# Sixteen of 52 pairs on GpSimd, with three double steps per block and column-split second products, in a two-layer graph kernel

## The chip, the cores and the metric

The kernel runs on one NeuronCore of a Trainium2 chip. The metric is device time in microseconds, the median of several runs. In the profile PE is TensorE (PEld its weight loads), ACT is ScalarE, DVE is VectorE, POOL is GpSimd and SP is the engine that issues most transfers.

## What is computed

The input is a node matrix x (3327 x 128) and an adjacency matrix of zeros and ones (3327 x 3327). Layer 0 is a normalised graph convolution with batch norm. Layer 1, which takes over 97% of the time, is attention with 128 "batches" d, eight components h and a bias of twice the adjacency:

```python
h = jnp.maximum(_layernorm(x, axis=-1), 0.0)
q = (h @ Wq.T).reshape(d, n, h_)      # d = 128, n = 3327, h_ = 8; k and v likewise
a = jnp.einsum('dnh,dmh->dnm', q, k) * scale
a = a + adj + adj
a = jax.nn.softmax(a, axis=2)
out = jnp.einsum('dnm,dmh->dnh', a, v)
x = x + out.reshape(n, h_ * d) @ Wo.T
```

So for each of 128 batches a 3327 x 3327 matrix of scores is formed, exponentiated and multiplied with v. The kernel takes no row maximum: the scores are bounded beforehand (a flag sends inputs for which they are not into another branch, which this input does not take), and the row sum comes out of the second product through a column of ones in v.

## The kernel before

Layer 1 is done in 32 groups of four batches. A group has seven blocks of columns n (six of 512 and one of 255), and a block runs over the 26 chunks of 128 rows m. One chunk for two of the four batches is a *pair*, so there are 52 pairs per block. A pair goes through a *first product* (two matmuls with 32 rows each, L725, into a PSUM tile `s` of two banks), an exponential, and a *second product* (two matmuls with 9 columns of v as weights, L604, into the block's accumulator `av`).

The bias is added in one of two ways. A *plain* pair goes through `add` (L815): VectorE adds the adjacency tile `at` and writes `d` (L818); later one ScalarE instruction exponentiates all plain pairs of the step (`late`, L854 to L856). A *weighted* pair goes through `weighted` (L825): ScalarE exponentiates straight out of PSUM (L828) into `f`, and GpSimd multiplies by exp(2 adj), read from a DRAM array `wd` as tile `wt` (L831). Chunks below `WC` = 19 are plain (38 pairs), the seven from 19 on are weighted (14 pairs).

A block is 13 steps of four pairs. Steps 0 to 11 have three plain pairs and one weighted; step 12 has two and two, a *double step*. Each engine works strictly in the order in which the program issues, and the order is written out by hand in L799 to L858. In a single step it is, in the letters used further on: R (first product of the weighted pair, then its L828 and L831), the `late` exponential of the step before, P0 (first product of the first plain pair, and its L818), the first half of the second products of the step three before (`second(0)`: two pairs, eight matmuls), the work that ends a block (`step`, one piece of `finish` per step: a copy of `av`, four transposes, the division, the store), P1, P2, the work beside (`beside`), the other half of the second products (`second(1)`). In the double step the second weighted pair stands where P2 is.

The tile `s` has three buffers of two PSUM banks, and the two accumulators take the other two banks. The names `at` (4 buffers), `wt` (3), `d` (4) and `f` (5) are in SBUF.

`beside` (L756) fits in two kinds of extra work: the q, k and v projections of a later group (six parts per group, `projection` L192) and the output product of the group before (three parts, `outputs` L242). A part has a TensorE piece, issued at step 7 or 10, a VectorE (and GpSimd) piece at step 8 or 11 and a store at 9 or 12.

The weights `wd` are made once, since they are the same for all batches. For the first `EARLY` = 3 blocks this happens ahead of the attention (`weigh_early` L439, called twice at L499 and once at L598). For the other four blocks it happens in group 0 (`more_weights` L734): during block y the weights of block y+1 are loaded, exponentiated and stored in up to four portions of two chunks, one action per step.

Of the kernel before, what the change touches and what calls it, by code (L numbers as in the profile page):

```python
# [12 lines left out]
AF = mybir.ActivationFunctionType  # L13
# [9 lines left out]
NC = 26  # L23
# [5 lines left out]
HALF = 0.5 / math.sqrt(D)  # L29
SAFE = 30.0  # L30
SU = NC // 2
WC = 19
CH = 4 * NP // D
NG = D // G
EARLY = 3

# [6 lines left out]
def tile_two_layer_gnn(  # L45
# [240 lines left out]
    with tc.tile_pool(name="l0", bufs=1) as l0, tc.tile_pool(  # L286
# [143 lines left out]
            if 0 <= i < NQ - 2 and 4 * i + 4 <= c:  # L430
                spread(i)
        weights = []
        for y, (n0, w) in enumerate(blocks[:EARLY]):
            a = ap.tile([P, 7 * NB], F32, name="a")
            a7 = a.rearrange("p (c n) -> p c n", c=7)
            nc.sync.dma_start(a7[:, :, :w], adjr[:, WC:, n0 : n0 + w])
            weights.append((a7, n0, w))

        def weigh_early():  # L439
            a7, n0, w = weights.pop(0)  # L440
            nc.scalar.activation(a7[:, :, :w], a7[:, :, :w], AF.Exp, bias=low, scale=2.0)
            nc.sync.dma_start(
                wd[:, :, n0 : n0 + w].rearrange("c p n -> p c n"), a7[:, :, :w]
            )

# [147 lines left out]
        for i in range(1, NQ):  # L595
            columns(i, i % 2 == 0)
        keep_columns(0, NQ)
        weigh_early()  # L598

# [50 lines left out]
    def attention():  # L652


        with tc.tile_pool(name="adj", bufs=4) as ap, tc.tile_pool(
# [17 lines left out]
            if True:  # L673
# [5 lines left out]
                def at(i):  # L679
                    return i * G  # L680

                def pairs(s):


                    last = s == SU - 1
                    plain = [(j // 2, j % 2) for j in range(3 * s, 3 * s + 3 - last)]
                    rest = [(WC + s // 2, 1 - s % 2)]
                    return plain, rest + ([(NC - 1, 0)] if last else [])


                wanted, have = [], {}
                for x, (i, y, s) in enumerate(steps):
                    n0, w = blocks[y]
                    for c, _ in pairs(s)[0]:
                        if (0, i, y, c // 2) not in have:
                            have[0, i, y, c // 2] = None
                            wanted.append((x, 0, i, y, c // 2))
                    c = pairs(s)[1][0][0]
                    if (1, i, y, c) not in have:
                        have[1, i, y, c] = None  # L700
                        wanted.append((x, 1, i, y, c))

                def fetch(x):
                    while wanted and wanted[0][0] <= x:
# [29 lines left out]
                def more_weights(i, y, s):  # L734

                    k, phase = s // 3, s % 3
                    if i or y + 1 >= len(blocks) or y + 1 < EARLY or k > 3:
                        return
                    n0, w = blocks[y + 1]
                    c = WC + 2 * k  # L740
                    n = min(2, NC - c)
                    if phase == 0:
                        have["w"] = wk.tile([P, 2, NB], F32, name="t4")
                        nc.sync.dma_start(
                            have["w"][:, :n, :w], adjr[:, c : c + n, n0 : n0 + w]
                        )
                    elif phase == 1:
                        a = have["w"][:, :n, :w]
                        nc.scalar.activation(a, a, AF.Exp, bias=low, scale=2.0)
                    else:  # L750
                        nc.sync.dma_start(
                            wd[c - WC : c - WC + n, :, n0 : n0 + w].rearrange("c p n -> p c n"),
                            have["w"][:, :n, :w],
                        )

                def beside(i, y, s):  # L756


                    for j in [1, 2] if i == 0 else [i + 2] if i + 2 < NG else []:
                        if (y, s) != (0 if i else 3 * (j - 1), 3):  # L760
                            continue
                        hj = wk.tile([P, CH], F32, name="hj")
                        nc.sync.dma_start(hj, hd[:, j * CH : (j + 1) * CH])
                        extra.extend(projections(wk, hj, j, False, ov, low_half[:CH, 1:2]))
                    if s in (8, 11) and extra:
                        drive(extra[0])
                    if s in (9, 12) and extra:
                        drive(extra.pop(0))
                    if s in (7, 10) and extra:
                        drive(extra[0], avs2[(i * len(blocks) + y + 1) % 2])  # L770
                    if (y, s) == (2, 12) and i:
                        extra.extend(outputs(wk, i - 1))

                extra = []

                def second(part):

                    (i, y, s), es = waiting[0]
                    n0, w = blocks[y]
                    av = avs2[(i * len(blocks) + y) % 2]  # L780
                    ps = sum(pairs(s), [])
                    for j in (0, 1) if part == 0 else (2, 3):
                        c, half = ps[j]
                        for x in range(2):
                            weigh(
                                sets[i % 2], av, w, es[j][:, x, :w], 2 * half + x, c,
                                s == 0 and part == 0, s == SU - 1 and part == 1,
                            )
                    if part:
                        waiting.pop(0)  # L790
                        if s == SU - 1:
                            ending.append(finish(rp, av, at(i), n0, w))

                def step():
                    for g in ending[:1]:
# [3 lines left out]
                for x, (i, y, s) in enumerate(steps):  # L799
                    n0, w = blocks[y]  # L800
                    fetch(x + PRE)
                    k = x - i * SU * len(blocks) - FROM[i]
                    if k == 0 and i + 1 < NG:
                        pending = loads(sets[(i + 1) % 2], at(i + 1))
                        total = len(pending)

                    while pending and (total - len(pending)) * (SU * len(blocks) - FROM[i] - 4) <= k * total:
                        pending.pop(0)()
                    more_weights(i, y, s)
                    due = len(waiting) == LAG  # L810
                    plain, rest = pairs(s)
                    d = ep.tile([P, 3, 2, NB], F32, name="d")
                    es = [d[:, j] for j in range(len(plain))]

                    def add(j, p):  # L815
                        c = plain[j][0]

                        nc.vector.scalar_tensor_tensor(  # L818
                            d[:, j, :, :w],
                            have[0, i, y, c // 2][:, c % 2, :w]  # L820
                            .unsqueeze(1).to_broadcast([P, 2, w]),
                            SAFE / 2, p[:, :, :w], ALU.min, ALU.add,
                        )

                    def weighted(c, half):  # L825
                        f = fp.tile([P, 2, NB], F32, name="f")
                        p = product(i, y, c, half)
                        nc.scalar.activation(  # L828
                            f[:, :, :w], p[:, :, :w], AF.Exp, scale=2.0
                        )  # L830
                        nc.gpsimd.tensor_tensor(  # L831
                            f[:, :, :w], f[:, :, :w],
                            have[1, i, y, c][:, :w].unsqueeze(1).to_broadcast([P, 2, w]),
                            ALU.mult,
                        )
                        es.append(f)

                    weighted(*rest[0])
                    if late is not None:
                        late()  # L840
                    add(0, product(i, y, *plain[0]))
                    if due:
                        second(0)
                    step()
                    add(1, product(i, y, *plain[1]))
                    if len(rest) > 1:
                        weighted(*rest[1])
                    else:
                        add(2, product(i, y, *plain[2]))
                    beside(i, y, s)  # L850
                    if due:
                        second(1)

                    def late(d=d, w=w, n=len(plain)):  # L854
                        flat = d[:, :n].rearrange("p j x n -> p (j x) n")[:, :, :w]
                        nc.scalar.activation(flat, flat, AF.Exp, scale=2.0)  # L856

                    waiting.append(((i, y, s), es))  # L858
                late()
                while waiting:  # L860
                    second(0)
                    step()
                    second(1)
                while ending:
                    step()
                for p, b in zip(outputs(wk, NG - 1), (0, 1, 0)):
# [197 lines left out]
```

## Time and profile before

| | |
|---|---|
| median of three runs | 10511.22 us (10510.94 to 10513.17) |
| time of the profiled execution | 10527.91 us |
| its span | 10526.1 us |
| mean granted TensorE clock | 0.986 |
| first L828 of the attention | 291.66 us after the start |
| group 0 (from its first L828 to that of group 1) | 377.1 us |
| groups 1 to 30, mean | 317.37 us |

A group of instructions is shown with its count, its busy time and the mean duration of one; behind the bar stands the idle time of the engine just before these instructions and what ended it. In the timeline the columns are the start in us, the duration, the engine, the line, the operation, tiles and shapes, and the number of instructions merged into the row. ScalarE instructions overlap: a row can start before the one above it has ended, so the distance of two starts is what an instruction costs when the engine is full.

### The profile page before, as it was taken

Reading aid. Unit: us, or ns where it says so; the run is one execution under the profiler, and the core shown is the slowest. Engines: PE = TensorE matmul, PEld = TensorE weight load, DVE = VectorE, ACT = ScalarE, POOL = GpSimd, SP = SyncE. Lnnn points to the kernel's source line nnn. Section 1 sums busy time; section 2 is a strip of 40 time slices with the busy share of each in tenths; the row PEclk is TensorE's granted clock in tenths of the full one; section 3 lists DMA queues with packets and bytes.
Section 4 is the critical chain, followed back from the end, with each engine's and each line's share of the span. In section 5 each row is a group of like instructions: output and inputs, shape, how many; then the busy total and the mean of one; then the engine's idle time right before and its main releaser. Section 6 shows DMA issues by size and latency. Waiting matters only on the chain. (4 is left out here: it accounts for less than half of the span.)

```text
span 10526.1 us, 186778 instructions
## 1 busy us (share of the span) xinstructions
PE 9922.7 (94%) x72399; PEld 2813.8 (27%) x72399; DVE 9714.9 (92%) x9949; ACT 9948.5 (95%) x6200; POOL 7497.1 (71%) x3868
## 2 busy tenths in 40 slices
PE   7889999999999999999999999999999999999999
PEld 3222222222222222222222222222222222222222
DVE  5789999999999999999999999999999999999998
ACT  4889999999999999999999999999999999999998
POOL 0667777777777777777777777777777777777776
PEclk8899999999999999999999999999999999999999
DMA  7655555555555555555555555555555555555554
GB/s 241 192 168 163 157 168 165 163 162 160 162 166 165 164 162 157 161 170 163 160 162 157 165 170 165 160 158 163 164 169 163 162 163 158 165 165 167 156 152 128
DMA packets 1115761, 1731.67 MB, mean 165 GB/s; under 512 B 198350, under 2 KB 441932, under 8 KB 1107180
## 3 DMA queue, kind: packets, MB, share of 16 engines
q1 hardware_dynamic: 1110478, 1713.99, 56.3%
q8 instruction: 568, 9.31, 0.4%
q10 hardware_dynamic: 4350, 5.64, 0.2%
q14 instruction: 333, 2.73, 0.1%
q0 software_dynamic: 32, 0.00, 0.0%
HBM read 1618.76 MB, written 100.53 MB: 163 GB/s over the span
## 5 line engine op out<-in xcount | busy, mean ns | idle before, releaser
L818 DVE SCALAR_TENSOR_TENSOR d<-at,s 128x1024 f32<-128x1024 f32 x8512 | 9204.3, 1138 | 642.7 <-PE s L725 406.2
L831 POOL TENSOR_TENSOR f<-f,wt 128x1024 f32<-128x1024 f32 (+1 forms) x3136 | 6983.8, 2235 | 2619.1 <-ACT f L828 2572.0
L856 ACT ACTIVATE d<-d 128x3072 f32<-128x3072 f32 (+1 forms) x2912 | 7372.9, 2532 | 73.4 <-DVE d L818 70.5
L604 PE MATMUL av<-d,v 128*9 128x512 f32 x34048 | 5528.5, 569 | 0.1
L725 PE MATMUL s<-q,k 32*128 32x512 f32 x23296 | 4280.7, 482 | 505.7 <-DVE d L818 218.0
L725 PEld LDWEIGHTS s<-q,k 32*128 32x128 f32 x23296 | 1773.9, 182 | 5829.2 <-DVE d L818 3312.2
L828 ACT ACTIVATE f<-s 128x1024 f32<-128x1024 f32 (+1 forms) x3136 | 3014.8, 970 | 313.8 <-PE s L725 252.3
L604 PE MATMUL av<-f,v 128*9 128x512 f32 x12544 | 2864.0, 571 | 0.0
L604 PEld LDWEIGHTS av<-d,v 128*9 128x9 f32 x34048 | 630.7, 88 | 1381.6 <-issue 1265.4
L604 PEld LDWEIGHTS av<-f,v 128*9 128x9 f32 x12544 | 310.6, 88 | 52.9 <-issue 41.0
L180 POOL CAST k<-ks 128x256 fp32r<-128x256 f32 x434 | 284.2, 655 | 0.0
L416 PE MATMUL acc<-a,A 128*128 128x512 f32 (+1 forms) x364 | 151.3, 568 | 24.0 <-ACT A L350 23.3
L619 PEld LDWEIGHTS av<-ident,avs 128*128 128x128 f32 (+1 forms) x864 | 121.1, 208 | 179.9 <-issue 178.8
L226 POOL TENSOR_TENSOR o<-pf,o 104x512 fp32r<-104x512 f32 x124 | 160.4, 1293 | 9.9
L619 PE MATMUL av<-ident,avs 128*128 128x128 f32 (+1 forms) x864 | 163.8, 311 | 0.6 <-DVE avs L612 0.6
L225 POOL CAST o<-pf 104x512 fp32r<-104x512 f32 x124 | 75.8, 611 | 115.3 <-DVE pf L224 59.8
L612 DVE COPY avs<-av 128x512 f32<-128x512 f32 (+1 forms) x224 | 144.2, 644 | 2.8 <-PE av L604 2.8
L423 DVE TENSOR_REDUCE amax<-a 128x1 f32<-128x3327 f32 x26 | 93.7, 3610 | 37.7 <-DMA a<-in_adj 37.7
L416 PEld LDWEIGHTS acc<-a,A 128*128 128x128 f32 x364 | 68.8, 192 | 108.8 <-issue 84.4
L420 ACT ACTIVATE junk<-a 128x3327 bf16<-128x3327 f32 x26 | 77.4, 2977 | 6.6 <-DMA a<-in_adj 6.5
L389 POOL TENSOR_TENSOR sq<-wk 128x512 f32<-128x512 f32 x2 | 2.1, 1040 | 102.3 <-PE aside L390 102.3
L629 DVE TENSOR_TENSOR oq<-av,ri 128x128 f32<-128x128 f32 (+1 forms) x224 | 64.1, 286 | 7.7
(120 smaller groups left out, 952.0 us busy)
## 6 DMA issues: line engine op xcount, KB each, us to landing
at<-in_adjT SPq DMA_DIRECT2D x1728, 512.0 KB
wt<-wd SPq DMA_DIRECT2D x1344, 256.0 KB
at<-in_adjT SPq DMA_DIRECT2D x288, 255.0 KB
ks<-kT SPq DMA_DIRECT2D x496, 104.0 KB
q<-qT SPq DMA_DIRECT2D x496, 104.0 KB
at<-in_adjT SPq DMA_DIRECT2D x192, 256.0 KB
a<-in_adj SPq DMA_DIRECT2D x26, 1663.5 KB
wt<-wd SPq DMA_DIRECT2D x224, 127.5 KB
```

Source lines behind the costliest of these rows:

```text
L180: nc.gpsimd.tensor_copy(k[:, c : c + n, half * 64 : half * 64 + 64], ks.bitcast(F32).rearrange("g (p c) -> g c p", c=NC)[:, c : c + n, :],)
L226: nc.gpsimd.tensor_tensor(o[:CH, 1], f[:CH], o[:CH, 0].bitcast(F32), ALU.subtract)
L416: nc.tensor.matmul(acc[i][:, :w], A[:, c, :], a[:, n0 : n0 + w], start=(c == 0), stop=(c == NC - 1),)
L423: nc.vector.tensor_reduce(amax[:, c : c + 1], a[:, :N], AX.X, ALU.max, apply_absolute_value=True)
L604: nc.tensor.matmul(av[32 * b : 32 * b + H + 1, :w], tiles[2][:, b, c, :], e, start=first, stop=last,)
L612: nc.vector.tensor_copy(avs[:, :w], av[:, :w])
L619: nc.tensor.transpose(pt[:R, j, :], avs[:, j : j + (R - 1) * J + 1 : J], ident)
L725: nc.tensor.matmul(p[:, x, :we], k[rs, c, :], q[rs, n0 : n0 + we], start=True, stop=True,)
L818: nc.vector.scalar_tensor_tensor(d[:, j, :, :w], have[0, i, y, c // 2][:, c % 2, :w] .unsqueeze(1).to_broadcast([P, 2, w]), SAFE / 2, p[:, ...
L828: nc.scalar.activation(f[:, :, :w], p[:, :, :w], AF.Exp, scale=2.0)
L831: nc.gpsimd.tensor_tensor(f[:, :, :w], f[:, :, :w], have[1, i, y, c][:, :w].unsqueeze(1).to_broadcast([P, 2, w]), ALU.mult,)
L856: nc.scalar.activation(flat, flat, AF.Exp, scale=2.0)
```

## The change

Three things change together.

First, `WC` becomes 18: 36 pairs are plain and 16 weighted. `DOUBLE` = (4, 8, 12) names three double steps, and `kinds` lists the pairs of each step (ten steps of three plain and one weighted, three of two and two). The list of wanted tiles takes all weighted chunks of a step. The extra work moves from steps 7/8/9 and 10/11/12 to 7/8/9 and 11/12/0 of the next block.

Second, in blocks wider than `NARROW` = 400 columns a second product is issued in two halves of the columns. `second(part, half)` replaces `second(part)`, and the order of a step is now: R, `late`, P0, `second(0, 0)` (a quarter of the second products), `step`, P1, P2 (or the second weighted pair), `beside`, `second(0, 1)`, `second(1, 0)`, `second(1, 1)`. In the block of 255 columns half 0 takes all columns and half 1 nothing.

Third, the early weights are now those of block 0 alone, in two tiles of half the columns. The third call of `weigh_early`, the last thing of the prologue, is gone, and `more_weights` makes the weights of blocks 1 to 6, so it also runs in blocks 0 and 1 of group 0. There are eight weighted chunks instead of seven, so its last portion has two chunks instead of one.

```diff
-WC = 19
+WC = 18
-EARLY = 3
+DOUBLE = (4, 8, 12)
+NARROW = 400
...
-        for y, (n0, w) in enumerate(blocks[:EARLY]):
+        for n0 in range(0, NB, NB // 2):
             a = ap.tile([P, 7 * NB], F32, name="a")
-            a7 = a.rearrange("p (c n) -> p c n", c=7)
-            nc.sync.dma_start(a7[:, :, :w], adjr[:, WC:, n0 : n0 + w])
-            weights.append((a7, n0, w))
+            a8 = a[:, : 8 * (NB // 2)].rearrange("p (c n) -> p c n", c=8)
+            nc.sync.dma_start(a8, adjr[:, WC:, n0 : n0 + NB // 2])
+            weights.append((a8, n0, NB // 2))
...
         keep_columns(0, NQ)
-        weigh_early()
...
+                kinds = []
+                for s in range(SU):
+                    j, k = (sum(len(x[i]) for x in kinds) for i in range(2))
+                    n = 2 if s in DOUBLE else 1
+                    kinds.append((
+                        [(x // 2, x % 2) for x in range(j, j + 4 - n)],
+                        [(WC + x // 2, 1 - x % 2) for x in range(k, k + n)],
+                    ))
...
-                    if i or y + 1 >= len(blocks) or y + 1 < EARLY or k > 3:
+                    if i or y + 1 >= len(blocks) or k > 3:
...
-                    if s in (8, 11) and extra:
+                    if s in (8, 12) and extra:
                         drive(extra[0])
-                    if s in (9, 12) and extra:
+                    if s == 9 and extra or s == 0 and (y or i) and begun:
                         drive(extra.pop(0))
-                    if s in (7, 10) and extra:
+                        begun.pop()
+                    if s in (7, 11) and extra:
+                        begun.append(1)
...
+                    h = w // 4 * 2 if w > NARROW else w
+                    n0, n1 = (0, h) if half == 0 else (h, w)
                     for j in (0, 1) if part == 0 else (2, 3):
-                        c, half = ps[j]
+                        if n0 == n1:
+                            break
+                        c, b = ps[j]
                         for x in range(2):
                             weigh(
-                                sets[i % 2], av, w, es[j][:, x, :w], 2 * half + x, c,
-                                s == 0 and part == 0, s == SU - 1 and part == 1,
+                                sets[i % 2], av[:, n0:n1], n1 - n0, es[j][:, x, n0:n1],
+                                2 * b + x, c, s == 0 and part == half == 0,
+                                s == SU - 1 and part == 1 and n1 == w,
                             )
...
                     add(0, product(i, y, *plain[0]))
-                    if due:
-                        second(0)
+                    second(0, 0)
                     step()
                     add(1, product(i, y, *plain[1]))
...
                     beside(i, y, s)
-                    if due:
-                        second(1)
+                    second(0, 1)
+                    second(1, 0)
+                    second(1, 1)
```

More of the change, by code (lines that the diff above doesn't have):

```diff
@@ L432, in tile_two_layer_gnn @@
         weights = []
-        for y, (n0, w) in enumerate(blocks[:EARLY]):
+        for n0 in range(0, NB, NB // 2):
             a = ap.tile([P, 7 * NB], F32, name="a")
-            a7 = a.rearrange("p (c n) -> p c n", c=7)
-            nc.sync.dma_start(a7[:, :, :w], adjr[:, WC:, n0 : n0 + w])
-            weights.append((a7, n0, w))
+            a8 = a[:, : 8 * (NB // 2)].rearrange("p (c n) -> p c n", c=8)
+            nc.sync.dma_start(a8, adjr[:, WC:, n0 : n0 + NB // 2])
+            weights.append((a8, n0, NB // 2))
         def weigh_early():
[L440 to L444, printed above, removed]
+            a8, n0, w = weights.pop(0)
+            nc.scalar.activation(a8, a8, AF.Exp, bias=low, scale=2.0)
+            nc.sync.dma_start(wd[:, :, n0 : n0 + w].rearrange("c p n -> p c n"), a8)
         top = l0.tile([P, 1], F32, name="top")
@@ L682, in pairs @@
                 def pairs(s):
[L685 to L688, printed above, removed]
+                    return kinds[s]
+                kinds = []
[6 more added lines that the diff above has]
+                    ))
                 wanted, have = [], {}
@@ L697, in attention @@
                             wanted.append((x, 0, i, y, c // 2))
[L698 to L701, printed above, removed]
+                    for c, _ in pairs(s)[1]:
+                        if (1, i, y, c) not in have:
+                            have[1, i, y, c] = None
+                            wanted.append((x, 1, i, y, c))
                 def fetch(x):
@@ L772, in beside, with second @@
                         extra.extend(outputs(wk, i - 1))
-                extra = []
-                def second(part):
+                extra, begun = [], []
+                def second(part, half):
+                    if not due:
+                        return
                     (i, y, s), es = waiting[0]
@@ L781, in second @@
                     ps = sum(pairs(s), [])
+                    h = w // 4 * 2 if w > NARROW else w
+                    n0, n1 = (0, h) if half == 0 else (h, w)
                     for j in (0, 1) if part == 0 else (2, 3):
-                        c, half = ps[j]
+                        if n0 == n1:
+                            break
+                        c, b = ps[j]
                         for x in range(2):
                             weigh(
-                                sets[i % 2], av, w, es[j][:, x, :w], 2 * half + x, c,
-                                s == 0 and part == 0, s == SU - 1 and part == 1,
+                                sets[i % 2], av[:, n0:n1], n1 - n0, es[j][:, x, n0:n1],
+                                2 * b + x, c, s == 0 and part == half == 0,
+                                s == SU - 1 and part == 1 and n1 == w,
                             )
-                    if part:
+                    if part and half:
                         waiting.pop(0)
                         if s == SU - 1:
-                            ending.append(finish(rp, av, at(i), n0, w))
+                            ending.append(finish(rp, av, at(i), blocks[y][0], w))
                 def step():
@@ L859, in attention @@
                 late()
+                due = True
                 while waiting:
-                    second(0)
+                    for j in range(4):
+                        second(j // 2, j % 2)
                     step()
-                    second(1)
                 while ending:
```

## The prediction

> **What bounds the kernel now.** I read the page first: four engines are between 71% and 95% busy, so shares decide nothing, and the question is which of them is never idle inside a step.
>
> ```profile
> span 10526.1 us, 186778 instructions
> PE 9922.7 (94%) x72399; PEld 2813.8 (27%) x72399; DVE 9714.9 (92%) x9949; ACT 9948.5 (95%) x6200; POOL 7497.1 (71%) x3868
> ```
>
> Then the timeline of ScalarE over a double step (the two merged L828 are its second one and the first of the next block):
>
> ```profile
> 5030.17 1.03 ACT L828 ACTIVATE f<-s 128x1024 f32<-128x1024 f32 x1
> 5031.07 2.78 ACT L856 ACTIVATE d<-d 128x3072 f32<-128x3072 f32 x1
> 5033.73 1.04 ACT L828 ACTIVATE f<-s 128x1024 f32<-128x1024 f32 x1
> 5034.63 2.79 ACT L856 ACTIVATE d<-d 128x3072 f32<-128x3072 f32 x1
> 5037.29 1.96 ACT L828 ACTIVATE f<-s 128x1024 f32<-128x1024 f32 x2
> 5039.10 1.95 ACT L856 ACTIVATE d<-d 128x2048 f32<-128x2048 f32 x1
> 5040.90 1.07 ACT L828 ACTIVATE f<-s 128x1024 f32<-128x1024 f32 x1
> ```
>
> The reader should see that there is no gap. By distances of starts an L828 costs 0.90, a long L856 2.66 and a short one 1.80. A single step is 0.90 + 2.66 = 3.56 us of ScalarE, a double one 3.61 (5037.29 to 5040.90). VectorE needs 3 x 1.137 = 3.41 in a single step (nine L818 lasted 10.27 us back to back) and 2.27 in a double one. So in the six wide blocks ScalarE sets the pace, and VectorE is 0.15 behind it.
>
> The waits then say what ScalarE loses, whole run:
>
> ```profile
> POOL f L831 <- ACT f L828: 2572.0, 2228, 4.1
> DVE d L818 <- PE s L725: 406.2, 785, 2.3
> ACT f L828 <- PE s L725: 252.3, 380, 7.6
> ACT d L856 <- DVE d L818: 70.5, 212, 0.6
> ```
>
> I added ScalarE's gaps in groups 1 to 31 by block and step: 11 us of a group's 317.4. Four places hold most of them: 1.68 at step 1, after the double step; 1.91 (0.26 to 0.35 per wide block) where `late` waits for VectorE at step 6, behind the work of `finish`; about 3.8 at steps 8 and 11, just behind the extra TensorE pieces (0.41 a projection, 1.33 the output product); 2.6 in the block of 255. That block runs at VectorE's pace (13 L818 in 8.79 us, 0.676 each, three per 2.03 us step).
>
> TensorE's order is the last view:
>
> ```profile
> 5034.07 0.50 PE L725 MATMUL s<-q,k 32*128 32x512 f32 x2
> 5034.82 0.50 PE L725 MATMUL s<-q,k 32*128 32x512 f32 x2 [0.26 <-ACT f L828]
> 5035.25 0.60 PE L604 MATMUL av<-d,v 128*9 128x512 f32 x2
> 5035.27 0.60 PE L604 MATMUL av<-f,v 128*9 128x512 f32 x2
> 5035.69 0.60 PE L604 MATMUL av<-d,v 128*9 128x512 f32 x2
> 5035.70 0.60 PE L604 MATMUL av<-f,v 128*9 128x512 f32 x2
> 5036.23 0.51 PE L725 MATMUL s<-q,k 32*128 32x512 f32 x4
> ```
>
> The fourth product of the step (5034.82) waits until L828 has emptied its PSUM buffer; then come the second products, and only then R of the next step, for which ScalarE's next L828 waits. This makes a loop: L828 1.04, release 0.05, product 0.43, second products 0.98, R 0.50, hand-over 0.10: 3.10 us. ScalarE gives it 3.56, so 0.46 is spare. TensorE itself needs 4 x 0.43 for products at worst (0.43 for two when they start together) and 2 x 0.98.
>
> **What the Trainium skill says.** "TensorE: Matmul & The Clock Gate", Back-to-back issue gap, makes the distance of matmuls proportional to columns plus a few ns; the trace agrees: a set of four second products takes 0.43 us at 512 columns and 0.22 at 255 (5100.63 to 5100.85). Its Part 3 says that matmuls in different parts of the array run together but strictly in order; here four start within 0.02 us, and the wait of one product holds all behind it. "TensorEngine Tiling", Key Properties, says that a change of tiling mode drains the array; I see 0.11 per batch of second products (0.98 against 2 x 0.43), twice a step before and after. "PSUM — Partial Sum Buffer", The four PSUM rules, says a start flag clears a whole zero region; so the start on half 0 alone serves both halves and adds no instruction. No run here shows that.
>
> **The change part by part**, per group of 1 to 31 unless said.
>
> *Pairs moved, ScalarE.* Two single steps become double: 2 x (3.61 - 3.56) = 0.10 per wide block: +0.6.
>
> *Pairs moved, VectorE.* Two L818 go per block. In wide blocks VectorE was behind only after `finish`; with a double step at 4 and 8 it gains 1.3 us each time, more than the 0.6 of the copy and 0.7 of the division. So the waits at step 6 go: 1.91 recorded, plus 0.11 each of lost overlap (the next ScalarE instruction could have started 0.11 before the end of the last): -2.6. What is late next is R. In the narrow block VectorE is the pace: -2 x 0.676 = -1.35.
>
> *Pairs moved, GpSimd.* It multiplies 16 instead of 14 times, 2.36 us each (three in 7.09): 37.8 of 46.4 us in a wide block, plus sorting (0.69 each) and projections (0.6 + 1.3, now in double steps). After a double step with a projection it is some 4 us late; its product is used three steps, 10 us, later. Cover enough: 0. If the cover were gone, each double step with a projection would cost up to 1.9.
>
> *Transfers.* Eight `wt` per block for seven, nine `at` for ten, half a megabyte more or less on queues busy 56%: 0.
>
> *Column split.* The matmuls themselves cost the same (0.22 twice for 0.43; at worst 0.01 for each of eight sets). What moves is the order: before P1 stand 0.54 us of second products instead of 0.98, and behind P2 stand 6 x 0.22 + 0.11 = 1.41 instead of 0.98. The loop becomes 3.53 of 3.56. A plain single step just fits (0, at worst 0.05), but the spare 0.46 is gone, and what used it is paid in full. Three things did.
>
> - Extra TensorE pieces stand in the loop (`beside` is ahead of the quarters): a projection of 1.03 us lost 0.41 + 0.11. Now it loses 0.43 more. Nine pieces per group: +3.9. Two of them, the transposes, cost nothing before and may cost less.
> - The step behind a double one. ScalarE asks for the next R after 0.90 + 1.80 = 2.70. The loop of 3.10 lost 0.40 where P2 waits for this L828; where P1 waits for the double step's second L828, 0.90 earlier, nothing. The waits on the weight loads show P2 bound to ScalarE in 120 of 192 such steps, to VectorE in 69; 0.4 x 120/192 = 0.25 agrees with the 1.68 over six blocks. After: 3.53 - 2.70 = 0.83 or nothing, three times a block. Which buffer a product takes is settled when the program is built; with VectorE less loaded I expect the ScalarE one in three of ten: 18 x 0.83 x 0.3 = 4.5, less 1.68 + 0.4 as now: +2.4. Bounds: -2.1 and +12.8.
> - The transposes of `finish` in step 4: now in a double step, where R may come 0.9 later: 0.
>
> Sum: 0.6 - 2.6 - 1.35 + 3.9 + 2.4 = +2.95; 31 groups: +91.
>
> *Group 0 and prologue.* Block 2 made weights and took 54.0 us, block 1 did not and took 48.3: 5.7 for blocks 0 and 1 each, +11.4. SP issues `at` and `wt` behind the store of weights, which waits for ScalarE; that is in this figure. Fourth portions of two chunks: 1.15 - 0.72 in four blocks, +1.7. In front, the first L828 waited 6.9 us for the store of the last early weights and VectorE until 298.2 for its first `at`; without 1.8 MB beside the 1.7 MB of `hd` I take -4 (bounds 0 and -8). Together +9.
>
> The profiled execution was 10527.91; + 91 + 9 is 10628. Its time lies 16.7 above the median, so about 10610 as runs are measured.
>
> **Rivals.**
> *Faster: the loop isn't closed.* If buffers are dealt so that P2 rarely waits for the same step's L828, the longer train behind P2 starts earlier and costs nothing. Then only the relief counts: 0.6 - 2.6 - 1.35 - 2.1 = -5.45, -169 in all, and 10350; with the extra pieces still dearer -1.55 and 10470. I take 10420. For it: 406 us of VectorE's waits on products, which a shorter stretch ahead of P1 is fit to remove. Against: in steps 2, 3, 5, 7, 8, 9, 11 the fourth product is bound to ScalarE in 98% of wide blocks. It decides if fewer than about half of the single steps close the loop.
> *Much slower: every double step closes it.* 18 x 0.83 - 2.1 = 12.8 instead of 2.4: +322 more, 10930.
> *GpSimd late.* 1.9 us in four places a group: 10840. Against: the 10 us of cover.
> *It cancels:* 10510, if buffers fall as the first rival has it in about half of the cases.
>
> **How the numbers follow.** The forecast has 0.50, much slower 0.16, GpSimd 0.06, faster 0.19, cancels 0.09. The predicted time is 10610. The range 10430 to 10860 leaves out half of the faster and most of the much slower case, about 0.2. A measurement of this kernel can tell 0.2%, 21 us. Faster by more: 0.19; within: 0.09; slower: 0.72. The likeliest case alone spans 10540 to 10760.
>
> **What would show it.** Right: the wait of L856 for VectorE nearly gone; the wait of L828 for TensorE up from 252 us to over 400, sitting behind steps 7 and 11 and behind double steps; L604 doubled in count for wide blocks at half the duration of a set; groups at about 320 us, group 0 near 387; VectorE busy about 9200. Wrong: groups below 315, with ScalarE without gaps behind the extra pieces; or GpSimd as what L604 or L828 waits for.

## The result: 5.65% slower

| | before | after |
|---|---|---|
| median | 10512.19 us (10510.94 to 10520.04, four runs) | 11105.14 us (11099.29 to 11120.36, four runs) |
| ratio | | 1.0565, interval 1.0546 to 1.0583 |
| profiled execution, span | 10526.1 us | 11099.0 us |
| groups 1 to 30, mean | 317.37 us | 336.27 us |
| first L828 (after: L842) | 291.66 us | 277.41 us |
| start of group 1 | 668.7 us | 659.2 us |

The forecast was 10610, with a range up to 10860; the time lies above it. Prologue and group 0 together became 9.5 us shorter, 30 groups took 567 us more and the last group with the end 15 more: 573, the whole difference of the spans.

The line numbers move: VectorE's addition is now L832, ScalarE's exponential from PSUM L842, `late` L870, the first product L729, the second L602. The page of the changed kernel:

```profile
span 11099.0 us, 267638 instructions
PE 9890.5 (89%) x112335; PEld 3785.3 (34%) x112335; DVE 9375.5 (84%) x9501; ACT 10011.2 (90%) x6655; POOL 8452.3 (76%) x4316
```

ScalarE's work grew by 63 us in a run that is 573 longer, and no other engine is busier than ScalarE. So the time went into waiting. The waits name where (whole run; the columns are the sum, the number and the longest):

```profile
DVE d L832 <- PE s L729: 1165.2, 1760, 4.7
PE s L729 <- ACT f L842: 1001.9, 2595, 2.2
ACT f L842 <- PE s L729: 842.0, 1002, 2.3
```

ScalarE's wait for TensorE went from 252 to 842 us, TensorE's for ScalarE from 172 to 1002. Each waits for the other: a loop. VectorE's waits, which the shorter stretch ahead of P1 might have cut, rose from 406 to 1165. The wait of `late` for VectorE fell from 70.5 to 10.5 us, as forecast.

ScalarE's timeline shows the place (group 16, block 1; the two merged L842 are the second one of the double step 4 and that of step 5):

```profile
5781.88 2.78 ACT L870 ACTIVATE d<-d 128x3072 f32<-128x3072 f32 x1
5784.54 1.95 ACT L842 ACTIVATE f<-s 128x1024 f32<-128x1024 f32 x2
5786.35 1.95 ACT L870 ACTIVATE d<-d 128x2048 f32<-128x2048 f32 x1
5788.99 1.02 ACT L842 ACTIVATE f<-s 128x1024 f32<-128x1024 f32 x1 [0.69 <-PE s L729]
```

Before, the L828 at 5040.90 in the same place followed with no gap (the mean gap there was 0.20 in blocks 1 to 5). TensorE in the same stretch:

```profile
5784.38 0.62 PE L602 MATMUL av<-d,v 128*9 128x256 f32 x8
5785.63 0.50 PE L729 MATMUL s<-q,k 32*128 32x512 f32 x2 [0.64 <-ACT f L842]
5786.55 0.50 PE L729 MATMUL s<-q,k 32*128 32x512 f32 x2 [0.41 <-ACT f L842]
5786.98 0.82 PE L602 MATMUL av<-d,v 128*9 128x256 f32 x10
...
5788.39 0.51 PE L729 MATMUL s<-q,k 32*128 32x512 f32 x4
```

P2 of step 5 (5786.55) waits for the L842 of its own step, which started at 5785.44 (the second of the two merged ones above); then three quarters of second products run until 5788.39; then comes R of step 6, and ScalarE takes it at 5788.99. The loop is 3.55 us, 0.02 from the working in the prediction. ScalarE had asked after 2.70.

This is the common case, but not the only one. In groups 1 to 31 there are 527 such steps, 17 a group (step 0 of block 0 stands behind the narrow block and loses nothing). From the L842 of R to that of the next R, 447 of them took 3.54 us on average. In the other 80 TensorE's granted clock was at half for at least 0.5 us, and they took 4.95. One of them (group 11, block 3, step 0, whose L842 starts at 4185.54), on TensorE and then on ScalarE:

```profile
4187.05 1.46 PE L602 MATMUL av<-d,v 128*9 128x256 f32 x10
```

```profile
4190.62 1.02 ACT L842 ACTIVATE f<-s 128x1024 f32<-128x1024 f32 x1 [2.26 <-PE s L729]
```

The stretch around that TensorE row (its bounds and length, the busy times of PE, PEld, DVE, ACT and POOL, then the granted clock, 0.50, and the transfers):

```profile
4187.00:4189.80 2.80, 2.80 (x30) 0.83 (x28) 1.59 (x2) 1.36 (x1) 2.80 (x2) 0.50 0.79 240
```

The ten matmuls that took 0.82 at 5786.98 take 1.46 here, and the step 5.08. By the trace's record of the clock, the changed kernel has 90 stretches at half clock after the start of group 1 (340 us), and 80 of them begin in a step behind a double one, 1.4 to 2.0 us after its L842; the kernel before has 26 (156 us). What lowers the clock there wasn't tried.

Gaps of ScalarE in groups 1 to 31, per group, added up by step from the trace, beside the terms of the forecast:

| term | forecast | measured |
|---|---|---|
| ScalarE's extra work | +0.6 | +0.6 (same durations) |
| `late` waiting for VectorE at step 6, wide blocks | -2.6 | -2.6 (1.91 to 0.00, and overlap) |
| block of 255 | -1.35 | +1.25 (29.14 to 30.39) |
| extra TensorE pieces (gaps at steps 8 and 12) | +3.9 | +3.6 (3.82 to 7.44) |
| behind double steps (gaps at steps 1, 6, 10) | +2.4 | +16.1 (16.2 recorded, 2.0 of lost overlap, less 2.1) |
| gap at step 4 of block 0 | none | -0.4 (0.85 to 0.43) |
| sum | +2.95 | +18.55, of 18.9 |

The last term goes with the clock: in the kernel before a stretch at half clock begins at step 2 of block 0 in 18 of the groups, in the changed kernel in 7.

### The profile page after: what moved, and what is told of

Read it like the earlier page. It is cut to its first block, busy times and chain, and to the rows that moved or that the text cites. A ratio compares the mean times of both kernels' runs of the same rounds, so it can differ in the third digit from the quotient of the medians.

```text
span 11099.0 us, 267638 instructions
## 1 busy us (share of the span) xinstructions
PE 9890.5 (89%) x112335; PEld 3785.3 (34%) x112335; DVE 9375.5 (84%) x9501; ACT 10011.2 (90%) x6655; POOL 8452.3 (76%) x4316
## 5 line engine op out<-in xcount | busy, mean ns | idle before, releaser
L832 DVE SCALAR_TENSOR_TENSOR d<-at,s 128x1024 f32<-128x1024 f32 x8064 | 8843.9, 1141 | 1560.0 <-PE s L729 1165.2
L845 POOL TENSOR_TENSOR f<-f,wt 128x1024 f32<-128x1024 f32 (+1 forms) x3584 | 7949.6, 2232 | 2360.6 <-ACT f L842 2352.2
L870 ACT ACTIVATE d<-d 128x3072 f32<-128x3072 f32 (+1 forms) x2912 | 7001.6, 2404 | 12.1 <-DVE d L832 10.5
L602 PE MATMUL av<-d,v 128*9 128x256 f32 x59904 | 5300.5, 387 | 0.1
L729 PE MATMUL s<-q,k 32*128 32x512 f32 x23296 | 4111.4, 484 | 1115.3 <-ACT f L842 1001.9
L842 ACT ACTIVATE f<-s 128x1024 f32<-128x1024 f32 (+1 forms) x3584 | 3376.0, 964 | 871.1 <-PE s L729 842.0
L729 PEld LDWEIGHTS s<-q,k 32*128 32x128 f32 x23296 | 1616.5, 183 | 4415.2 <-ACT f L842 2134.6
L602 PE MATMUL av<-f,v 128*9 128x256 f32 x26624 | 2926.0, 387 | 0.0
L602 PEld LDWEIGHTS av<-d,v 128*9 128x9 f32 x59904 | 1445.0, 90 | 2278.6 <-issue 1393.4
L602 PEld LDWEIGHTS av<-f,v 128*9 128x9 f32 x26624 | 1071.1, 92 | 257.5 <-issue 8.7
```

The costliest lines, as they stand in the source:

```text
L602: nc.tensor.matmul(av[32 * b : 32 * b + H + 1, :w], tiles[2][:, b, c, :], e, start=first, stop=last,)
L729: nc.tensor.matmul(p[:, x, :we], k[rs, c, :], q[rs, n0 : n0 + we], start=True, stop=True,)
L832: nc.vector.scalar_tensor_tensor(d[:, j, :, :w], have[0, i, y, c // 2][:, c % 2, :w] .unsqueeze(1).to_broadcast([P, 2, w]), SAFE / 2, p[:, ...
L842: nc.scalar.activation(f[:, :, :w], p[:, :, :w], AF.Exp, scale=2.0)
L845: nc.gpsimd.tensor_tensor(f[:, :, :w], f[:, :, :w], have[1, i, y, c][:, :w].unsqueeze(1).to_broadcast([P, 2, w]), ALU.mult,)
```

## The experiments

Theory 1 is the loop, closed behind every double step because P2 is given the PSUM buffer that ScalarE empties. The rivals: the doubled number of matmuls and weight loads slows TensorE by itself (theory 2); GpSimd's two more multiplications come late (theory 3). A kernel that was timed once has no interval; the kernel before took 10504 to 10527 us beside these.

**Pairs alone, undivided, old order.** The edit to the changed kernel:

```diff
-NARROW = 400
+NARROW = NB
...
                     second(0, 0)
+                    second(0, 1)
                     step()
...
                     beside(i, y, s)
-                    second(0, 1)
                     second(1, 0)
                     second(1, 1)
```

> The changed kernel with the second products undivided and in the old order (half of them ahead of P1, half behind P2); pairs, double steps, extra work and prologue as changed. Theory 1 (the loop L828, P2, second products, R, L828, closed behind every double step by P2 taking ScalarE's buffer): the loop is 3.10 again, 0.40 over the 2.70 of a double step plus 0.11 of lost overlap, 18 times a group; about 10700 us (10600 to 10760). Theory 2 (the doubled number of matmuls and weight loads makes TensorE slow): back near or below the kernel before, 10350 to 10500, since the division is gone. Theory 3 (GpSimd's 16 multiplications come late): stays at 11100.

Measured 10463.53, against 10508.55 of the kernel before beside it. Theory 3 falls: GpSimd does all 16 multiplications here, and the kernel is faster than before. The time fits theory 2, and theory 1 as it was put is off by 240 us.

**Division and order alone, on the kernel before.** `second(part, half)` and the new order, everything else as before.

> The kernel before with the second products divided and in the new order alone; 38 plain pairs, one double step, extra work and prologue as before. Theory 1: six double steps a group lose about 1.0 instead of 0.35, the extra pieces 0.43 more each: +7 us a group, about 10740. Theory 2: the whole loss, 11000 to 11100. Theory 3: as before, 10510.

Measured 10733.7: theory 1's number. The gap behind the one double step was 0.86 in blocks 1 to 5 (0.20 before), and that at a projection 0.82 (0.41; averages over groups 1 to 31, the last two of which have no projections).

**Division with the old order.** As the first run, with `NARROW` = 400.

> The changed kernel with the second products divided but in the old order (two quarters ahead of P1, two behind P2). It differs from the first run in this list in the division alone, from the changed kernel in the order alone. Theory 1: within 30 us of the first run, about 10700. Theory 2: 11050 to 11100. Theory 3: 11100.

Measured 10619.87. This is neither: 156 us above the first run by the division alone, but 485 below the changed kernel by the order alone. The traces tell why. The weight load in front of a product carries the wait for its PSUM buffer, either ScalarE's semaphore or VectorE's. In the first run P2 was bound to ScalarE in step 5 (191 of 192 wide blocks), but to VectorE in step 0 (158) and step 9 (189), and only step 6 showed a gap of this kind (0.26). With the division it is ScalarE in all three (192, 190, 191), and the gaps are 0.28, 0.27 and 0.32 at steps 1, 6 and 10. Eleven such gaps more per group, at 0.30 and 0.11 of lost overlap, are 4.5 us; the groups differ by 5.0 (315.8 and 320.8). So the first run was no test of theory 1: its buffers had been dealt otherwise, which I had not foreseen.

**Another buffer for P2.** The changed kernel with the buffers dealt by hand:

```diff
-name="psc", bufs=3, space=PSUM
+name="psc", bufs=1, space=PSUM
...
+                order = [0, 1, 2]
-                def product(i, y, c, half):
+                def product(i, y, c, half, skip=0):
...
-                    p = psc.tile([P, 2, NB], F32, name="s")
+                    order.append(order.pop(skip))
+                    p = psc.tile([P, 2, NB], F32, name=f"s{order[-1]}")
...
-                        add(2, product(i, y, *plain[2]))
+                        add(2, product(i, y, *plain[2], int(s - 1 in DOUBLE or s == 0 and x > 0)))
```

> The changed kernel, order and division unchanged, but the three PSUM buffers of the first product dealt by hand: always the one used longest ago, only P2 of the step behind a double step takes the next one, which VectorE has emptied, and leaves ScalarE's to the R behind it. Theory 1: the stalls behind double steps (18 of 1.0 us a group) go, about 10560 to 10620, with the stalls behind the extra pieces left. Theories 2 and 3: 11050 to 11100, since nothing but the wait is changed.

Measured 10630.37: 475 us gone with no instruction changed. ScalarE behind a double step (its L845 is the exponential from PSUM, L873 is `late`):

```profile
5547.54 2.79 ACT L873 ACTIVATE d<-d 128x3072 f32<-128x3072 f32 x1
5550.21 1.96 ACT L845 ACTIVATE f<-s 128x1024 f32<-128x1024 f32 x2
5552.01 1.96 ACT L873 ACTIVATE d<-d 128x2048 f32<-128x2048 f32 x1
5553.98 1.02 ACT L845 ACTIVATE f<-s 128x1024 f32<-128x1024 f32 x1
```

The last row has no gap. On TensorE:

```profile
5551.30 0.74 PE L732 MATMUL s<-q,k 32*128 32x512 f32 x4 [0.64 <-ACT f L845]
5551.97 0.82 PE L602 MATMUL av<-d,v 128*9 128x256 f32 x10
...
5553.38 0.51 PE L732 MATMUL s<-q,k 32*128 32x512 f32 x4
5553.81 0.62 PE L602 MATMUL av<-d,v 128*9 128x256 f32 x8
```

P1 and P2 now run as one row: the wait ahead of them is for the double step's second exponential, and the three quarters end 2.28 us after the L845 of 5551.10, not 2.95 as in the changed kernel. The gaps at steps 1, 6 and 10 are 0.01 to 0.04 on average in blocks 1 to 5, and the steps ahead of them take 2.81 to 2.89 us, near the 2.70 after which ScalarE asks. Those at a projection stay at 0.83. The stretches at half clock are gone as well: 9 are left after the start of group 1, none of them behind a double step, though the instructions are the same.

**The control.** The same dealing by hand without the exception (`skip` always 0).

> Control for the fourth run: the changed kernel with the three buffers dealt by the same hand, but always the one used longest ago, so P2 behind every double step waits for ScalarE, as in the changed kernel. Theory 1: the time of the changed kernel, 11100 (within 40). Rival (dealing by hand changes something else, and that was the gain of 475 us): about 10630.

Measured 11098.03, with the same two cases behind a double step: 480 of 527 at 3.54 us, 47 at 4.94. Dealing by hand changes nothing in itself; which buffer P2 takes behind a double step is worth 468 us.

**Undivided with dealt buffers, and divided with dealt buffers.** The first and the third run with the buffers of the fourth.

> The first run (pairs as changed, second products undivided, old order) with the buffers of the first product dealt by hand as in the fourth: P2 behind a double step takes VectorE's. Theory 1 (buffers): in the first run the steps behind the double step 4 alone had P2 on ScalarE's buffer and lost 0.27 + 0.11, six times a group; they go: 313.5 us a group, about 10390. Rival (the choice of buffers is a symptom, TensorE is simply short of time behind a double step): no change, 10460.

> The run before in this list with the second products divided by columns, in the old order, with the buffers dealt by the same hand. Theory 1 (the division costs TensorE nothing, it only shifted which buffer a product was given when the program was built; the third run lost 156 us to the first that way): within 15 us of the run before, about 10390. Rival (twice as many matmuls and weight loads cost time by themselves): 100 to 160 us above it, about 10500 to 10550.

Measured 10409.91 and 10408.97. The groups of second products, first undivided, then divided (count, busy us, mean ns):

```profile
L602 PE MATMUL av<-d,v 128*9 128x512 f32 x32256 | 5058.6, 566 | 0.1
```

```profile
L602 PE MATMUL av<-d,v 128*9 128x256 f32 x59904 | 5078.2, 381 | 0.1
```

Nearly twice the matmuls are busy 0.4% longer and the run is not longer at all. Theory 2 falls: in this order the division costs nothing, and the 156 us of the third run were buffers. The undivided kernel was timed again, four times:

> The undivided kernel with dealt buffers once more, timed in rounds: 10410, ratio 0.990.

Measured 10412.5, ratio 0.9897 (0.9881 to 0.9914).

What the buffers do, in one table (P2 behind the double step bound to ScalarE, in wide blocks of 192; gaps of ScalarE in blocks 1 to 5):

| kernel | second products behind P2 | P2 bound at steps 0 / 5 / 9 | gap at 1 / 6 / 10, us | group, us |
|---|---|---|---|---|
| changed | 1.41 us | 191 / 190 / 191 | 1.00 / 0.92 / 0.82 | 336.3 |
| control | 1.41 | dealt: all | 0.87 / 0.82 / 0.76 | 336.0 |
| another buffer | 1.41 | dealt: none | 0.01 / 0.04 / 0.01 | 320.7 |
| divided, old order | 0.98 | 192 / 190 / 191 | 0.28 / 0.27 / 0.32 | 320.8 |
| pairs alone | 0.98 | 34 / 191 / 3 | 0.00 / 0.26 / 0.00 | 315.8 |
| undivided, dealt | 0.98 | dealt: none | 0.00 / 0.00 / 0.00 | 313.95 |
| divided, old order, dealt | 0.98 | dealt: none | 0.00 / 0.00 / 0.00 | 313.96 |

**The front alone.** The kernel before with weights of one block in front (two halves), the others in group 0.

> The kernel before with the prologue's part of the change alone: weights of block 0 in two halves in front, those of blocks 1 to 6 during group 0, chunks from 19 on as before. From the changed kernel's trace: the attention starts 14 us earlier and group 0 takes 5 to 12 us more: 10497 to 10510. As predicted: 4 us earlier and 13 more, 10518.

Measured 10515.07; the kernel before beside it had 10525.65, too near to tell by one time of each. By the trace the attention starts 13.9 us earlier, group 0 takes 10.2 more and group 1 begins 3.7 earlier.

**Extra pieces in double steps.** On the undivided kernel with dealt buffers: TensorE's part at 8 and 12, VectorE's at 9 and 0.

> The first run of this list with the TensorE pieces of the extra work in the double steps 8 and 12 instead of the single steps 7 and 11, VectorE's in 9 and 0, stores in 10 and 1. Theory 1: in a double step R of the next step is wanted 0.9 later, so a piece of 1.03 no longer delays ScalarE: 3 to 3.8 us a group less, about 10280 to 10310. Rival (a piece costs its TensorE time wherever it stands): unchanged, 10390; if VectorE, with no slack in single steps, comes late with its pieces: 10390 to 10420.

Measured 10434.58, no gain: 25 us above the undivided kernel with dealt buffers, and 15 above the highest of the rival's figures, which had been reckoned from 10390 for that kernel and not from the 10410 that it took. The gaps at steps 8 and 12 went to zero, and the projections left none behind the double steps, as theory 1 has it. But waits of 0.11 to 0.24 came up at steps 1, 4, 6 and 10, and 0.43 and 0.50 at steps 9 and 10 by the output product. VectorE's pieces now stand in single steps, where it has little to spare; the waits at step 4 are for VectorE itself, those at the other steps for TensorE, and that VectorE is behind them too is likely but not shown.

**Quarters 2, 1, 1.** Two quarters ahead of P1, one between P1 and P2, one behind, with dealt buffers.

> The changed kernel with buffers dealt as in the fourth run and another order of the quarters: two ahead of P1, one between P1 and P2, one behind P2. Theory 1: the train behind P2 is 0.54 instead of 1.41, a projection piece of 1.03 in it makes the loop 1.04 + 0.05 + 0.43 + 1.03 + 0.54 + 0.50 + 0.10 = 3.69 against 3.56: it costs 0.25 instead of 0.53 in the old order; about 2.2 us a group below the undivided kernel with dealt buffers, 10340. Rival (P2 comes later for VectorE, which has no slack in single steps): 10410 to 10450.

Measured 10551.32, ratio 1.0036: a miss, and not for the rival's reason alone. At an extra piece (L266 is the output product):

```profile
5014.03 0.50 PE L732 MATMUL s<-q,k 32*128 32x512 f32 x2
5014.47 0.62 PE L602 MATMUL av<-f,v 128*9 128x256 f32 x8
5015.02 0.50 PE L732 MATMUL s<-q,k 32*128 32x512 f32 x2
5015.45 2.00 PE L266 MATMUL av<-wo,t 128*104 128x128 f32 x16
```

P1 at 5014.03 and P2 at 5015.02 each take 0.43 to the next row. Side by side, as in the row at 5553.38 above (the next starts at 5553.81), two products take 0.43 together, since they use different rows of the array (the Trainium skill, "TensorE: Matmul & The Clock Gate", Part 3, says that such matmuls run concurrently). So the quarter between them costs TensorE 0.43, and the gap at step 8 behind a projection was 0.70 where the undivided order had 0.42. A group takes 4.8 us more than undivided (318.7); the gaps at steps 8 and 12 are 1.6 of that and the block of 255 another 1.1. The rest is spread over the wide blocks, and how much of it comes from the parted products and how much from VectorE getting P2 later was not separated.

**Extra piece ahead of P1.** The undivided kernel with dealt buffers and this edit:

```diff
                     step()
+                    if s in (7, 11) and extra:
+                        begun.append(1)
+                        drive(extra[0], avs2[(i * len(blocks) + y + 1) % 2])
                     add(1, product(i, y, *plain[1]))
```

(the same three lines are taken out of `beside`).

> The undivided kernel with dealt buffers and one edit: the TensorE piece of the extra work ahead of P1 instead of behind P2, outside of the loop. Theory 1: it fills the wait of TensorE for P2's buffer (0.26 to 0.7 us); P1 and P2 still start together; R comes 3.85 us after the L828 instead of 4.1 against 3.56 granted, so a piece costs 0.4 instead of 0.53 or less; 1 to 2 us a group: 10350 to 10385. Rival (VectorE gets P1 1.0 later and has no slack in single steps): 10410 to 10480.

Measured 10354.47, ratio 0.9843 (0.9826 to 0.9859): the fastest, faster than both kernels of this study. Its gaps at step 8 are 0.29 instead of 0.42 for a projection, at step 12 none. ScalarE's wait for TensorE over the run, of the undivided kernel with dealt buffers and of this one:

```profile
ACT f L845 <- PE s L732: 201.0, 356, 2.8
```

```profile
ACT f L842 <- PE s L732: 152.1, 262, 1.5
```

The two kernels were not timed beside each other, but each beside the kernel before. Of the 51 us between their profiled executions (10411.3 for the one timed again, 10359.9 for this), 35 lie in groups 1 to 30 (313.9 to 312.75 each) and 16.5 ahead of group 1.

## Why the prediction was wrong

*ScalarE as the pace, and the loop.* Right. The loop was worked out as 3.53; it is 3.54 on average at the full clock, and a step behind a double one that waits for nothing takes 2.70 (2.705 in the undivided kernel with dealt buffers). The trace, the control and the other-buffer run show it.

*Column split costs TensorE nothing.* Right: 10409.91 and 10408.97.

*The step behind a double one.* This step failed, in one term: "I expect the ScalarE one in three of ten". It was 190 or 191 of 192, three times a block. What such a step costs at the full clock was right: 0.83 forecast, and 3.54 less 2.70 measured (0.7 of it shows as a gap, the rest is lost overlap). The 80 steps at half clock lost 2.24 each, and for those the prediction had nothing: 80 x (4.95 - 3.54) is 113 us, or 3.6 a group. So 18 x 0.83 x 0.3 = 4.5 became 18.2 us a group. The prediction says itself that the buffer is settled when the program is built, and still takes its share from VectorE having less to do; nothing it shows ties the two. The waits are fixed in the instructions: with the division alone they changed in steps 0 and 9 (first and third run), at the same work. What rule the dealing follows wasn't tried. I had the bound (+12.8 for this term, 10930 for the run) as a rival at 0.16, and it is the mechanism that happened. The 175 us above it are in the main the half clock and the block of 255. One reading of the trace before was off as well: of the 1.68 that the prediction puts behind the double step, 0.69 stands at step 1 of block 0, behind the narrow block, and stays in every kernel here but the one with quarters 2, 1, 1.

*Block of 255.* The sign was wrong. It was reckoned from VectorE's pace, but its first steps still carry second products of the wide block ahead: the gaps at steps 2 and 3 rose from 0.29 and 0.62 to 0.90 each, with the order alone as well (the second run). Then three double steps bring gaps of their own (0.50 and 0.55 at 6 and 10). With L870 and L842 narrower by half, ScalarE asks sooner, which is the likely reason why the same train costs more.

*`late` and VectorE.* Right (-2.6), and the extra pieces right (+3.6 for +3.9).

*GpSimd.* Right: busy 8452, 13% more, and no wait for it among the large ones; the first run's 10463 has the same work on it.

*Prologue and group 0.* Forecast +9, measured -9.5 in the changed kernel and -3.7 with the front alone. The attention's first exponential starts 14.3 us earlier, not 4: beside the store that was taken away, the k tiles for group 0 landed 5 us sooner (POOL's L582 starts at 258.98, L583 had started at 263.99; why isn't shown). The second step starts only 4.3 earlier, since ScalarE then waits 16.5 us for the first weights. The rest is that blocks 3 to 5 of group 0, which had made weights before as well, took 55.0 to 61.5 us instead of 60.8 to 63.2; with the front alone they took 57.7 to 64.9.

*The point from which the faster rival decides* ("fewer than about half of the single steps close the loop") did not come: P2 is bound to ScalarE in single steps 2, 3, 7, 10 and 11 in over 95% of the wide blocks. But plain single steps cost nothing, as worked out: steps 1, 2 and 3 of blocks 1 to 5 take 3.56 to 3.58 us, before 3.56 to 3.57.

## What to carry to other kernels

When a matmul in an ordered queue waits for a PSUM buffer, ask who empties that buffer, and add up the loop from that instruction through everything queued behind the wait to its own next operand; compare it with the shortest time in which the engine comes round, not the usual one. Read the buffers' owners from the waits in the trace of the new build, since a change that leaves the work alone can deal them anew, and deal them by hand where it matters. Look at the granted clock of the stretches that wait, too: here a closed loop came with a lower one, and cost more than its sum. Work that stands between a wait and the next operand of the busiest engine belongs ahead of the wait, so long as it doesn't part matmuls that run side by side.

## What the runs showed of the hardware

- The profile shows each matmul of a second product as two, so a pair has four. A set of four with 256 columns, in different column groups, takes 0.22 us, with 512 columns 0.43: two half-width sets cost no more than one (10408.97 and 10409.91), although each matmul brings its own weight load.
- Two first products in different row groups take 0.43 us together when they start within 0.02 us and 0.43 each when second products stand between them (5553.38, and 5014.03 with 5015.02).
- Each gap of ScalarE costs 0.11 to 0.13 us more than it shows, since back-to-back instructions overlap by that much (in the prediction's view, rows of 1.03 and 2.78 us are followed after 0.90 and 2.66).
- TensorE's granted clock fell to half in stretches of mostly 3.4 us though TensorE was busy for 89% of the run. With the loop closed behind double steps there were 90 of them after the start of group 1 (76 in the control), with the same instructions and another buffer for P2 there were 9. A set of 256 columns took 0.43 us in them instead of 0.22.
